# Layer 1's matrices made by halves inside the spectrum's periods, and the weights' products of taps in six instructions

## The chip, the core and the metric

The kernel runs on one NeuronCore of a Trainium2 chip. The metric is the device time of one execution in microseconds; the median of three runs of the kernel before is 4494.61 (4492.34 to 4499.99). The profiled execution spans 4483.5 us. The core's engines are TensorE (PE; PEld is its weight load), VectorE (DVE), ScalarE (ACT), GpSimd (POOL) and SyncE (SP), which issues the transfers. Everything is in fp32.

## What is computed

The input x has the shape (4, 256, 256, 64). Layer 0 is a spectral block with a convolution behind it; layer 1 is a moving average plus a filter of the low frequencies along one axis, which is linear in x.

```python
# layer 0
h  = pw(layernorm(x), w_te)                     # 64 -> 128 channels
F  = fft2(h)
fc = gelu(pw(concat(real(F), imag(F)), w_fc))   # 256 -> 256
x1 = x + pw(real(ifft2(fc)), w_tp)              # 128 -> 64
d  = gelu(depthwise3x3(pw(layernorm(x1), w_fe), w_dw) + b_dw)
x2 = x1 + pw(d, w_fp)
# layer 1, along axis 1 of x2, for each of the 64 channels c
trend = moving_average(x2, 25)
xf    = rfft(x2 - trend)[:128]
out   = trend + irfft(einsum(xf, w_real[c] + 1j * w_imag[c]))
```

Because layer 1 is linear along its axis, the kernel makes one 256x256 matrix per channel from `w_real[c]`, `w_imag[c]` and the average, and applies it by matmul at the end. There are 64 such matrices. They depend on the weights alone, so that their place in the program is free until layer 1 begins. The depthwise 3x3 convolution and the 1x1 convolution ahead of it are joined in the same spirit: the weights `wc_main` and `wc_half` are products of `w_fe` with sums and differences of the taps of `w_dw`. They too depend on weights alone, and are needed from the first chunk of the convolution on.

## The kernel before

**A matrix of layer 1** takes four operations, defined in `matrices`. `v` (L1108, L1109) is two matmuls with 512 columns into one PSUM bank, one with the real and one with the imaginary weights; `vc` (L1113) copies the bank to SBUF on ScalarE; `mm` (L1119) is four matmuls with 256 columns; `mt` (L1130) adds the average's table `avgT` on VectorE and sends the matrix to DRAM (`m_d`, L1131). In a trace each fp32 matmul has two records.

**The order.** The instructions of TensorE, VectorE, ScalarE and GpSimd stand in an order that is written out by hand; each engine works through its own in order. An order is a text of names; `do(op, k)` brings an operation up to index k, after the ones it follows. A number behind a colon is added to the index of the turn or period. SyncE's transfers are not in these orders: a load takes its place there as soon as its buffer is to be had.

The program has these stages:

- **The starting stage**: 17 turns of the order FIRST. A turn takes two chunks of the first image through the layer norm and the forward transform along the rows (`fl` load, `fq` to `fp` statistics, `fx` scaling on GpSimd, `fa`, `fb`, `fh0`, `fh1` sums and differences, `y0`, `y1` matmuls L435, `yt` copies), and makes three matrices, 51 in all.
- **The weights' pieces**: `prepare` is a generator, whose pieces are taken one at a time. From turn 1 on, FIRST takes one at its head and one in its middle (behind `fm:1`, entry 22 of 44). The pieces of the convolution's weights are copies and sums of taps (L317 to L327), then 24 products (L338), each one instruction of 64x128. The last piece, with the bias and the edges (L344 to L365), is run behind the turns.
- **Between**: four steps, BETWEEN, with one matrix each (51 to 54), beside the last chunks of the starting stage.
- **The spectrum**: periods n = 35 to 70. A period takes one chunk of the forward transform and two pairs of columns through the spectrum: `x` (L540, the transform of the columns), `xs` (L555, copy on ScalarE), `m0`, `m1` (L564, the products with the joined weights), `gc` (L578), `b` (L583), `g` (Gelu, L587), `p` (L593, GpSimd), `z` (L617), `zs`, `w` (L634), `zt`; and one step back: `u` (L666), `us` (L683), `uc` (L696), `uf` (L715). The first `us` copy belongs to n = 38. At n = 35 `yr` (L512) prepares the first, special pair.
- **Periods with and without matrices**: n = 35 to 45 use the order SPECTRUM_AND_MATRIX, which holds one matrix per period (numbers 55 to 63, the operations of one matrix drawn out over two periods). From n = 46 to 70 the order is SPECTRUM, which has no matrices. The pools of the matrices and of `prepare` are closed at n = 46, and the convolution's pool is opened in their place. With that the six first loads of `x_c` (L821) may start.
- **The convolution** beside the spectrum of the next images, from n = 71 on, in the order FULL, and at last **layer 1**, which reads the matrices.

**PSUM** is one pool of eight banks, taken in rotation; the ninth request waits for the readers of the first.

Of the kernel before, what the change touches and what calls it, by code (L numbers as in the profile page):

```python
# [129 lines left out]
def conv_seq_kernel(ctx: ExitStack, tc: tile.TileContext, a: dict, tables: bass.AP, out: bass.AP):  # L130
# [108 lines left out]
    def prepare(prep):  # L239
# [76 lines left out]
        tap = lambda dy: w_dwb.rearrange("p (y x) o -> p y x o", x=3)[:, dy]  # L316
        nc.vector.tensor_copy(w_dwh[:, :, 0], tap(0))  # L317
        nc.vector.tensor_copy(w_dwh[:, :, 3], tap(2))
        yield
        w_mid = prep.tile([P, 3, HID], F32, tag="w_mid", name="w_mid")  # L320
        w_sum = prep.tile([P, 3, HID], F32, tag="w_sum", name="w_sum")
        yield
# [5 lines left out]
        for dst, lo, dx in (  # L328
            (wc_main[0:C, 0], 0, 1),
            (wc_main[C:P, 0], C, 2),  # L330
            (wc_main[0:C, 1], 0, 0),
            (wc_main[C:P, 1], C, 1),
            (wc_half[0:C], 0, 2),
            (wc_half[C:P], C, 0),
        ):
            for k in range(4):
                yield
                nc.vector.tensor_tensor(  # L338
                    dst[:, k], w_feg[lo : lo + C], w_dwh[lo : lo + C, dx, k], ALU.mult
                )  # L340
        yield

        ps = bank("ps_b9")
# [739 lines left out]
    def matrices(pool):  # L1083
# [44 lines left out]
        def third(c):  # L1128
            mt = pool.tile([P, 2, N], F32, tag="mt", name=f"mt_{c}", bufs=3)
            nc.vector.tensor_tensor(mt.rearrange("p t n -> p (t n)"), avgT, pss.pop(c), ALU.add)  # L1130
            nc.sync.dma_start(m_d[c], mt)  # L1131

        load(0)
        return {"v": first, "vc": between, "mm": second, "mt": third}


    CM, CO = 2, 2
# [64 lines left out]
    for b in range(B):  # L1202
# [14 lines left out]
        T0 tt0 tt1 eh:-2 | T1 tt0 tt1 gh:-2 | gm T1 | gh gm T1:1 | em T0 | eh em T0:1  # L1217
        gc_0 gh o1:-2 | gc_1 gh o1:-2 | cf0 gc_0 | cf1 gc_1 | ce0 eh cf0 cf1 | ce1 ce0 | cE ce1
        a0 cE | a1 cE | o0 a0 a1 | o1 a0 a1 | fs0 o0 ft0:-1 | fs1 o1 ft1:-1 | ft0 fs0 | ft1 fs1
        st0 ft0 | st1 ft1 | vc v | mm vc | mt mm  # L1220
    """

    def numbered(text):

        return [(w.split(":")[0], int(w.split(":")[1]) if ":" in w else 0) for w in text.split()]

    follows = {}
    for line in FOLLOWS.replace("\n", "|").split("|"):
# [17 lines left out]
        fx:1 vc:2 vc:1 yt0:-1 yt1:-1  # L1246
    """)

    SPECTRUM_AND_MATRIX = numbered("""
        x:1 fq g1:-1 x z:-2 xs:1 zs:-2 v xs fl:1 p1:-1 w:-2 vc b0:-1 fr fm zt:-2 g0:-1 p0:-1 m0 m1  # L1250
        gc1 y1:-2 u b1 z:-1 gc0 fx:-1 b0 zs:-1 y0:-2 fR g1 w:-1 us fM yt1:-2 fa:-1 g0 mm:-1 m1:1 uc
        p1 m0:1 fb:-1 yt0:-2 gc1:1 b1:1 gc0:1 p0 fh1:-1 mt:-1 fp uf fh0:-1 zt:-1
    """)

    SPECTRUM = numbered("""
        fr m0:-1 x g1:-1 xs p1:-1 gc0:-1 x:1 fq m0 z:-2 b0:-1 y1:-2 xs:1 fm gc0 m1 fR zs:-2 g0:-1
        gc1 w:-2 fx:-1 fl:1 y0:-2 fM zt:-2 b0 p0:-1 fp z:-1 fa:-1 fb:-1 yt1:-2 fh1:-1 u b1 yt0:-2
        zs:-1 us fh0:-1 uc m1:1 w:-1 g0 gc1:1 b1:1 p0 zt:-1 g1 p1 uf
        UL:1 XL:1
    """)  # L1260
    PAIRS = set("x xs m0 m1 gc0 gc1 b0 b1 g0 g1 p0 p1 z zs w zt".split())
    BACK = {"u", "us", "uc", "uf"}
    MATRICES = {"v", "vc", "mm", "mt"}

    BETWEEN = [
        numbered("fl:1 fq fr fR"), numbered("fm fM fp"), numbered("fa:-1 fb:-1 fh0:-1 fh1:-1"),
        numbered("fx y0:-2 y1:-2 yt0:-2 yt1:-2"),
    ]
    AHEAD = len(BETWEEN)
    BESIDE = C - 3 * (S0 // 2) - AHEAD  # L1270

    ops, done = {}, {}

    def do(op, index):

        if op not in ops:
            return
        for k in range(done.get(op, -1) + 1, index + 1):
            for other, at in follows.get(op, ()):
                do(other, k + at)  # L1280
            done[op] = k
            if op in PAIRS:
                if k < B * KH:
                    ops[op](k)
            elif op in BACK:
                ops[op](k)
            elif op in MATRICES:
                if k < C:
                    ops[op](k)
            elif op in forward:  # L1290
                if k < B * FWD:
                    ops[op](k)
            elif k in chunk_at:
                ops[op](chunk_at[k])

    def period(n):
        if any(n - k in chunk_at for k in range(5)):
            names = FULL
        else:
            names = SPECTRUM_AND_MATRIX if n - S0 < BESIDE + 2 else SPECTRUM  # L1300
        for op, at in names:
            base = n
            if op in PAIRS:
                base = 2 * (n - S0)
            elif op in BACK:
                base = n - S0
            elif op in MATRICES:
                base = n - S0 + C - BESIDE
            do(op, base + at)

    def starting(n, prep):

        for i, (op, at) in enumerate(FIRST):
            do(op, (3 if op in MATRICES else 2) * n + at)
            if n and i % (len(FIRST) // 2) == 0:
                next(prep, None)

    with in_order, ExitStack() as right:
        with (
# [7 lines left out]
            with ExitStack() as early:  # L1327
# [12 lines left out]
                do("yt0", FWD - 1)  # L1340
                do("yt1", FWD - 1)
                load_group(0)
                for k, names in enumerate(BETWEEN):
                    do("v", C - BESIDE - AHEAD + k)
                    do("vc", C - BESIDE - AHEAD + k)
                    do("mt", C - BESIDE - AHEAD + k - 1)
                    for op, at in names:
                        do(op, S0 - 1 + at)
                begin(0)
                ops |= spectrum  # L1350
                for n in range(S0, S0 + BESIDE + 2):
                    period(n)
                do("mt", C - 1)
            conv = right.enter_context(tc.tile_pool(name="conv", bufs=2, side="right"))
            ops |= convolution(conv)
            for n in range(S0 + BESIDE + 2, S0 + opened(B - 1) + 2):
                period(n)
        with tc.tile_pool(name="seq", bufs=1, side="left", reuse_waits="tile") as seq:
            mts = [matrix_load(seq, c) for c in range(0, CG, CM)]
# [51 lines left out]
```

## Time and profile before

| | us |
|---|---|
| median of three runs | 4494.61 |
| span of the profiled execution | 4483.5 |
| first and last product of the weights' taps | 92.8, 276.8 |
| `x` of n = 35, first records and the bulk | 311.2, 313.1 |
| `x` of n = 39 | 374.8 |
| `us` of n = 39 | 387.4 |
| `us` of n = 46 | 501.4 |
| `us` of n = 66 | 780.4 |
| `us` of n = 71 | 885.7 |

The page gives for each engine its busy time over the span, and the busy share in 40 slices of 112 us each. The timeline gives single instructions; the idle time ahead of one stands in brackets with the instruction that ended it. From `us` to `us` is one period: 16.0 us from n = 39 to 45, then 18.1 and 14.2, then 13.9 to 14.0 up to n = 66.

### The profile page before, as it was taken

The page shows a single profiled execution, that of the slowest core. Times are in us where ns is not written, and L with a number is a line of the kernel's source. Part 1 is how long each engine was busy: PE and PEld are TensorE (multiplying, and loading weights), DVE is VectorE, ACT ScalarE, POOL GpSimd, SP SyncE. Part 2 cuts the span into 40 slices and gives each one's busy share as a digit, 9 for nine tenths or more (in the row PEclk, how much of TensorE's full clock was granted, in tenths as well). Part 3 has the DMA queues.
Part 4 walks back from the last instruction along what each step waited for, and adds up shares of the span by engine and source line. Part 5 has one row for each costly group of instructions (what it writes and reads, how often), then busy time and mean ns, then how long its engine had stood idle before and what let it go on. Part 6 is the DMA issues. An engine that isn't in the chain of part 4 may idle for free.

```text
span 4483.5 us, 63463 instructions
## 1 busy us (share of the span) xinstructions
PE 4346.1 (97%) x22347; PEld 2220.4 (50%) x22347; DVE 3588.9 (80%) x5483; ACT 2508.6 (56%) x3686; POOL 2773.1 (62%) x1774
## 2 busy tenths in 40 slices
PE   7999999799999999999999999999999999999999
PEld 4444333355555555455555555555555455554444
DVE  7988999899999999999998777777777788862222
ACT  2337788666666666666666666666664334331111
POOL 6868899787777777877777555555554555530000
PEclk9999999999999999999999999999999999999999
DMA  6654655444444444444444333333334333329887
GB/s 189 203 178 134 182 151 152 131 114 134 135 134 135 135 128 137 118 132 132 132 132 118 109 108 95 108 99 95 109 104 144 114 95 91 102 89 332 323 321 270
DMA packets 756581, 655.00 MB, mean 146 GB/s; under 512 B 40141, under 2 KB 649375, under 8 KB 747944
## 3 DMA queue, kind: packets, MB, share of 16 engines
q1 hardware_dynamic: 756264, 650.95, 48.0%
q8 instruction: 178, 2.92, 0.3%
q14 instruction: 139, 1.14, 0.1%
HBM read 364.81 MB, written 286.00 MB: 145 GB/s over the span
## 4 chain that ended last, share of the span: by engine, by line
PE 83%; DVE 6%; POOL 4%; DMA 3%; ACT 2%; issue 2%; SPq 1%; DVEq 0%; ACTq 0%; POOLq 0%
PE ps_h_c L915 19%; PE ps_h_c L934 11%; PE ps_o L1166 9%; PE ps_p L564 9%; PE ps_f_c L990 5%; PE ps_z L617 5%; PE ps_s_c L832 5%; PE ps_u L666 4%; PE ps_x L540 4%; PE ps_y L435 4%; PE ps_t_c L869 3%; PE ps_ft_c L1011 3%; PE ps_zt L634 2%; POOL xb L429 1%; DMA xc<-x_d 1%
## 5 line engine op out<-in xcount | busy, mean ns | idle before, releaser
L593 POOL TENSOR_TENSOR g<-g 128x512 f32<-128x512 f32 (+1 forms) x520 | 736.6, 1428 | 545.3 <-ACT g L587 545.3
L915 PE MATMUL ps_h_c<-td_c,wc_main 128*128 128x512 f32 x2048 | 921.7, 593 | 0.0
L583 DVE TENSOR_TENSOR g<-ps_p,g 128x512 f32<-128x512 f32 x1040 | 692.2, 682 | 43.0 <-ACT g L578 25.0
L587 ACT ACTIVATE g<-g,b_fc 128x1024 f32<-128x1024 f32 (+1 forms) x520 | 586.0, 1147 | 181.5 <-DVE g L583 179.8
L230 POOL TENSOR_TENSOR rstd_c<-var_c,minus_half 128x16 f32<-128x16 f32 x128 | 371.8, 2905 | 466.7 <-DVE var_c L224 456.0
L578 ACT COPY g<-ps_p 128x512 f32<-128x512 f32 (+1 forms) x520 | 301.2, 583 | 462.4 <-PE ps_p L564 446.1
L915 PEld LDWEIGHTS ps_h_c<-td_c,wc_main 128*128 128x128 f32 x2048 | 369.1, 190 | 369.8 <-issue 303.7
L934 PEld LDWEIGHTS ps_h_c<-td_c,wc_half 64*128 64x128 f32 x4032 | 417.0, 187 | 244.4 <-issue 194.4
L564 PE MATMUL ps_p<-xs,wp 64*128 64x512 f32 (+1 forms) x2080 | 513.7, 601 | 23.3 <-ACT xs L555 23.3
L934 PE MATMUL ps_h_c<-td_c,wc_half 64*128 64x128 f32 (+1 forms) x4032 | 515.3, 392 | 4.3 <-POOL td_c L889 4.3
L1166 PE MATMUL ps_o<-xc,mt 128*128 128x512 f32 x1024 | 444.5, 596 | 16.4 <-DMA xc<-x_d 16.4
L230 POOL TENSOR_TENSOR rstd<-var,minus_half 128x16 f32<-128x16 f32 x128 | 382.3, 2987 | 77.6 <-DVE var L224 77.6
L966 DVE TENSOR_TENSOR h_c<-h_c,ps_h_c 128x512 f32<-128x512 f32 x512 | 317.3, 682 | 125.8 <-PE ps_h_c L934 125.7
L983 ACT ACTIVATE h_c<-h_c,b_conv 128x1024 f32<-128x1024 f32 x256 | 280.3, 1145 | 203.3 <-DVE h_c L979 203.2
L1180 DVE TENSOR_SCALAR oc<-ps_o,b_fp 128x512 f32<-128x512 f32 x128 | 96.1, 751 | 362.7 <-PE ps_o L1166 355.8
L429 POOL TENSOR_TENSOR xb<-xt 128x512 f32<-128x512 f32 x224 | 290.4, 1313 | 97.9 <-DVE xt L422 96.2
L959 DVE TENSOR_TENSOR h_c<-h_c,ps_h_c 128x512 f32<-128x512 f32 x256 | 175.6, 686 | 199.2 <-PE ps_h_c L934 189.2
L1166 PEld LDWEIGHTS ps_o<-xc,mt 128*128 128x128 f32 x1024 | 195.1, 191 | 265.2 <-issue 237.9
L540 PEld LDWEIGHTS ps_x<-tab,yb 128*64 128x64 f32 x4064 | 242.9, 139 | 130.5 <-issue 95.0
L617 PE MATMUL ps_z<-g,w_tp 128*64 128x512 f32 x1024 | 280.6, 610 | 22.8 <-POOL g L593 21.8
L1178 ACT ACTIVATE oc<-ps_o,b_fp 128x512 f32<-128x512 f32 x128 | 87.9, 687 | 374.3 <-PE ps_o L1166 273.4
L564 PEld LDWEIGHTS ps_p<-xs,wp 64*128 64x128 f32 x2080 | 196.8, 187 | 178.0 <-issue 123.8
(138 smaller groups left out, 7757.2 us busy)
## 6 DMA issues: line engine op xcount, KB each, us to landing
y_d<-yt SPq DMA_DIRECT2D x256, 256.0 KB, 2.5
yb<-y_d SPq DMA_DIRECT2D x256, 256.0 KB, 3.5
u_d<-ut SPq DMA_DIRECT2D x256, 256.0 KB, 4.3
x_c<-in_x_dram SPq DMA_DIRECT2D x128, 512.0 KB, 5.7
x_d<-st SPq DMA_DIRECT2D x128, 512.0 KB, 4.8
xc<-x_d SPq DMA_DIRECT2D x64, 1024.0 KB, 7.1
out_dram<-oc SPq DMA_DIRECT2D x256, 256.0 KB, 3.8
xt<-in_x_dram SPq DMA_DIRECT2D x504, 128.0 KB, 2.8
```

The costliest lines, as they stand in the source:

```text
L230: nc.gpsimd.tensor_tensor(rstd, var, minus_half.to_broadcast([P, n]), ALU.pow)
L429: engine.tensor_tensor(sums[j][:, i], x0, x1, (ALU.add, ALU.subtract)[i])
L540: nc.tensor.matmul(ps[r * C : (r + 1) * C, j * N + t * P : j * N + (t + 1) * P], blk[:, t, k, r * C : (r + 1) * C], tb[:, t, :], start=Tru ...
L564: nc.tensor.matmul(ps[:, :nf], wp[rows, cols], rhs[rows], start=True, stop=r == 1 or not pr["special"],)
L583: nc.vector.tensor_tensor(gt[:, i], re, gt[:, 1], op)
L587: nc.scalar.activation(g, g, AF.Gelu, bias=b_fc[:, half : half + 1])
L593: nc.gpsimd.tensor_tensor(g[:, 0], g[:, 0], g[:, 1], op)
L617: nc.tensor.matmul(ps[r * C : (r + 1) * C, :nf], w_tp, d[:, :nf], start=True, stop=True)
L915: nc.tensor.matmul(ps, wc_main[:, par, k, :], ts[(*j, k)].rearrange("p j i -> p (j i)"), start=True, stop=False,)
L934: nc.tensor.matmul(pss[k, par][:, s * P : (s + n) * P], wc_half[lo : lo + C, k, :], ts[(*at_q, k)][lo : lo + C, at : at + n, :].rearrange( ...
L966: nc.vector.tensor_tensor(g, g, m, (ALU.add, ALU.subtract)[r])
L1166: nc.tensor.matmul(ps[:, :nf], mts[i // CM][:, i % CM, t, to * P : (to + 1) * P], xc[:, t, :, :, i, :], start=t == 0, stop=t == 1,)
```

## The change

It has two parts. The first spreads the matrices over the spectrum. SPECTRUM_AND_MATRIX is dropped, and all periods from n = 35 to 70 use SPECTRUM. Into it come four new operations, which make half a matrix: `hv` two matmuls with 256 columns (one half `t` of the matrix), `hc` a copy of 128x256, `hm` two matmuls with 256 columns, `ht` an addition of 128x256 and a transfer of 128 KB. A half takes two periods: `hv` and `hc` in the first, `hm` and `ht` in the second. So eight matrices, 56 to 63, are made in 32 periods and one more. BETWEEN gets a fifth, empty step, which makes matrix 55, and the matrices begun there are ended there. The pools of the matrices and of `prepare` now stay open up to n = 67.

The second part is for the starting stage: the four products of each block of the convolution's weights become one instruction of 64x512, with `w_feg` repeated along the free axis, and two other pieces are joined. FIRST takes a piece only in its middle, one per turn, so that all pieces are done within the turns.

```diff
-        yield
         w_mid = prep.tile([P, 3, HID], F32, tag="w_mid", name="w_mid")
...
-            for k in range(4):
-                yield
-                nc.vector.tensor_tensor(
-                    dst[:, k], w_feg[lo : lo + C], w_dwh[lo : lo + C, dx, k], ALU.mult
-                )
+            yield
+            nc.vector.tensor_tensor(
+                dst,
+                w_feg[lo : lo + C].unsqueeze(1).to_broadcast([C, 4, HID]),
+                w_dwh[lo : lo + C, dx],
+                ALU.mult,
+            )
...
+        def first_half(k):
+            c, t = C - BESIDE + k // 2, k % 2
...
+            ps = pss["h", k] = bank(f"ps_v_{c}_{t}")
+            for i, f in enumerate((f1, f2)):
+                nc.tensor.matmul(
+                    ps[:, :N],
+                    w[c - c % CG, i][:, c % CG, :],
+                    f.rearrange("p (r n) -> p r n", n=N)[:, :, t * P : (t + 1) * P],
+                    start=i == 0,
+                    stop=i == 1,
+                )
...
+        def second_half(k):
+            vs, ps = vss.pop(("h", k)), bank(f"ps_m_h_{k}")
+            for r, ic in enumerate((icr, ici)):
+                nc.tensor.matmul(ps[:, :N], vs[:, r], ic, start=r == 0, stop=r == 1)
...
+        st0 ft0 | st1 ft1 | vc v | mm vc | mt mm | hc hv | hm hc | ht hm
...
     SPECTRUM = numbered("""
-        fr m0:-1 x g1:-1 xs p1:-1 gc0:-1 x:1 fq m0 z:-2 b0:-1 y1:-2 xs:1 fm gc0 m1 fR zs:-2 g0:-1
+        hv hm fr m0:-1 x g1:-1 xs p1:-1 ht gc0:-1 x:1 fq hc m0 z:-2 b0:-1 y1:-2 xs:1 fm gc0 m1 fR
...
-        numbered("fx y0:-2 y1:-2 yt0:-2 yt1:-2"),
+        numbered("fx y0:-2 y1:-2 yt0:-2 yt1:-2"), [],
     ]
-    AHEAD = len(BETWEEN)
-    BESIDE = C - 3 * (S0 // 2) - AHEAD
+    BESIDE = C - 3 * (S0 // 2) - len(BETWEEN)
...
-            elif op in MATRICES:
-                base = n - S0 + C - BESIDE
+            elif op in HALF_MATRICES:
+                base = (n - S0 - HALF_MATRICES[op]) // 2
...
-            if n and i % (len(FIRST) // 2) == 0:
+            if n and i == len(FIRST) // 2:
                 next(prep, None)
...
+                do("mt", C - BESIDE - 1)
                 begin(0)
                 ops |= spectrum
-                for n in range(S0, S0 + BESIDE + 2):
+                early_end = S0 + 4 * BESIDE + 1
+                for n in range(S0, early_end):
                     period(n)
-                do("mt", C - 1)
```

## The prediction

> **What bounds the kernel now.** First the page's shares and slices: TensorE has records in 97% of the span, and VectorE stays near 90% up to slice 22. The edit lies in slices 1 to 8, where both rows are high, so the share of the whole span settles nothing.
>
> ```profile
> PE 4346.1 (97%) x22347; PEld 2220.4 (50%) x22347; DVE 3588.9 (80%) x5483; ACT 2508.6 (56%) x3686; POOL 2773.1 (62%) x1774
> PE   7999999799999999999999999999999999999999
> DVE  7988999899999999999998777777777788862222
> ```
>
> Next the busy time of each engine by stage. The columns are the window, its length, then PE, PEld, DVE, ACT and POOL busy, granted clock, DMA share, GB/s. I cut the windows at successive `us` copies (one per period); row 1 is one turn of the starting stage, rows 2 and 3 are periods in the order SPECTRUM_AND_MATRIX (row 3 after the matrices ran out), row 4 holds the change of order, row 5 is a period in the order SPECTRUM.
>
> ```profile
> 206.00:221.40 15.40, 14.40 (x53) 7.63 (x52) 14.98 (x24) 5.76 (x10) 12.76 (x7) 1.00 0.71 212
> ...
> 403.40:419.40 16.00, 15.95 (x94) 7.63 (x93) 14.35 (x22) 12.57 (x21) 12.75 (x8) 1.00 0.52 154
> ...
> 467.30:483.30 16.00, 14.03 (x90) 6.80 (x90) 14.35 (x22) 11.98 (x20) 12.75 (x8) 1.00 0.47 140
> 483.30:501.40 18.10, 14.77 (x78) 5.32 (x76) 15.57 (x21) 11.95 (x21) 16.55 (x9) 0.81 1.04 327
> ...
> 557.40:571.40 14.00, 13.11 (x82) 5.28 (x84) 13.28 (x20) 11.94 (x19) 13.22 (x9) 1.00 0.50 139
> ```
>
> The reader is to see that the two orders differ by 2 us a period, and that the longer one stays at 16.00 even without matrix work (row 3): TensorE fills 15.95 us where there is such work, and after it the chain of waits through the order itself holds the pace. The short order is nearly balanced: 13.1 to 13.3 us on TensorE, VectorE and GpSimd in 14.0 (mean 13.95).
>
> Last the timeline of one short period (start, duration, engine, operation; in brackets the idle time before it and who ended it):
>
> ```profile
> 560.00 1.97 PE L540 MATMUL ps_x<-tab,yb 128*64 128x128 f32 x32
> ...
> 562.20 0.57 ACT L555 COPY xs<-ps_x 128x512 f32<-128x512 f32 x1
> ...
> 562.82 1.13 PE L564 MATMUL ps_p<-xs,wp 64*128 64x512 f32 x4 [0.85 <-ACT xs L555]
> ...
> 565.77 0.77 DVE L217 SCALAR_TENSOR_TENSOR var<-total 128x16 f32<-128x16 f32 x1
> ...
> 568.59 1.29 DVE L402 TENSOR_TENSOR xb<-xt 128x512 f32<-128x512 f32 x2 [0.52 <-PE ps_y L435]
> ```
>
> TensorE has one hole of 0.85 us a period, between `x` and the first `m`; otherwise it runs end to end. The hole isn't made by `x`: its first half ends near 561.0, and `xs` starts at 562.20 because two Gelus hold ScalarE from 559.89 to 562.29. So matmuls placed ahead of `x` can push `x` later into this hole.
>
> **What the Trainium skill says.** "Perfetto Trace Analysis", Optimization Strategy, advises interleaving regimes that contend for different engines; here the trace shows only 0.85 us of room per period, so whether it pays is a matter of place. "SBUF — State Buffer", Who interferes with whom: a VectorE instruction with two SBUF inputs and a GpSimd instruction that reads SBUF exclude each other, one input from PSUM doesn't. The trace agrees for the weights' products and the scaling L237; the product ends with it (94.62 and 94.47):
>
> ```profile
> 92.57 1.90 POOL L237 TENSOR_TENSOR xt<-xt,rstd 128x1024 f32<-128x1024 f32 x1
> ...
> 92.78 1.84 DVE L338 TENSOR_TENSOR wc_main<-w_feg,w_dwh 64x128 f32<-64x128 f32 x1
> ```
>
> An unblocked product took 0.28 (101.03), while `mt` (avgT and PSUM) never exceeds 0.69. "VectorE: DVE Perf Modes", The TRN2 errata, gives (N+151)/0.96 ns for an fp32 tensor_tensor: 691 at N=512, and L402 shows 691 on average.
>
> **Part 1: the weights' products, starting stage.** Out: 24 of 64x128, 16 with mean 973 and 8 with mean 854 = 22.4 us of VectorE. In: 6 of 64x512. Each stands in the middle slot of a turn, the one where L237 blocks (92.78); the cheap slot at the head of the turn is dropped. Bounds for one: 0.69 free (L422's row, and the page's formula), 0.69 + 1.56 (1.84 less 0.28) = 2.25 blocked. I take blocked, 13.5, since the slot is the same: 9 us less VectorE. Each remaining turn is also near TensorE's floor: three matrices at 3.75 (below) and four `y` of 0.93 are 15.0, while turns take 15.4 to 17.6. So only part comes through. The last piece (b9, edges), which now stands alone behind the stage and takes TensorE from 286.86 to 289.53, moves into turn 13; its round trip over VectorE costs there about what it cost (the hole was 0.77). I take **-5** for the stage, range -12 to 0.
>
> **Part 2: one more matrix ahead of the spectrum.** `v` starts its two matmuls 0.96 apart (441.49, 442.45): 1.92. `mm` runs 450.96 to 452.78: 1.82. The fifth BETWEEN step has nothing beside it, and a drain follows: TensorE gets `v` 55, `mm` 54 and `mm` 55 = 1.92 + 2 x 1.82 = 5.56 before `x` of the first period, which now waits from 309.2 for `yr`, itself behind `mt` on VectorE. I take **+5.5** in full; 4 if the drain overlaps.
>
> **Part 3: spectrum periods, the main term.** Of the order with matrices 11 periods vanish; all 36 use SPECTRUM, 33 with a half step. Even periods add `hv` and `hc`, odd ones `hm` and `ht`. TensorE: `hm` is half an `mm`, 0.91; `hv` is two matmuls of 256 columns, 0.91 by the `mm` rate, up to 0.96 by `v`. In-order TensorE then has 13.1 + 0.91 = 14.0 us. They stand ahead of `m0:-1` and `x`: first `x` ends at 561.0 + 0.91 = 561.9, before `xs` can start at 562.20; both `x` end near 562.9, and `m0` starts 0.1 late instead of 0.9. Queued behind them is all of TensorE, hence this check decides.
>
> ScalarE gets `hc`, 128x256 from PSUM: 0.35 (`xs` at 256 columns is 0.352), every other period behind the square, and finds the idle 0.30 ahead of L578 at 564.99. VectorE gets `ht`, 0.42 (L422 at 128x256 is 0.416), every other period ahead of `b0:-1`. L217 further on is held 0.6 us by L237 anyway (0.77 against a median of 0.175), so the delay is swallowed there; the 0.52 ahead of L402 is a second reserve. Banks: each period takes 18 of the 8 rotating PSUM banks, now 19. The new one is reused by `y1`, which must wait for `hc` (about 564.55) or `ht` (563.8), and starts at 564.8: no wait.
>
> So 13.95 becomes 14.05 (14.2 if VectorE's mean +0.2 shows). From the `us` of n = 39 (387.4) to that of n = 66 (780.4) are 27 periods and 393.0 us; after, 27 x 14.05 = 379.4: **-13.6**. Ahead of that, `x` at 313.1 to `x` of n = 39 at 374.8 is 61.7 for four filling periods; at 14.4 each 57.6: **-4**.
>
> **Part 4: what the freed pool starts.** The conv pool opens at n = 68 instead of 46, and with it the six `x_c` loads of 512 KB. Row 4 above is that burst (327 GB/s): 18.1 + 14.2 against 2 x 13.95 is 4.4 us, which part 3 has counted as gone. It returns beside the second image's `yr` and the convolution's start: **+4**, from 0 (hidden in the gaps of 796 to 910, where TensorE is busy 91.5 of 114) to 12 if `xt` and `yb` queue behind it in SyncE's order.
>
> Sum: -5 + 5.5 - 13.6 - 4 + 4 = -13.1, so 4494.6 becomes **4481.5**. From n = 71 on nothing changes.
>
> **The rivals.**
> A, the forecast: hole filled, 4481.5.
> B, the half steps add their full 0.91 because `xs` is released by the Gelus, and these by TensorE's delayed `m`: a period of 14.86, 27 x 14.86 = 401.2, +8.2 in place of -13.6; with no gain while filling, +8.2 - 5 + 5.5 + 4 = +12.7, **4507, slower**. Against it: the Gelu ahead of `xs` hangs on `m1:1` at 557.30, which stands ahead of `hv`.
> C, the gain comes but the burst costs 12 at the convolution's start: -5, 4489.5. For it: the critical chain passes through the `xt` loads (2.2 us) in nearly every short period, so they have no slack.
> D, the starting stage falls to TensorE's floor (-12) and the burst hides (0): -24, 4470.5.
>
> **How the numbers follow.** Chances: A 0.52, B 0.12, C 0.20, D 0.16. The bound of 0.2% is 9 us: below 4485.6 lie D and nearly all of A, 0.66; C and the rest of A are within, 0.22; B is above, 0.12. The range takes in A with its unknowns, C, and D down to 4469, and leaves B out: 4469 to 4497.
>
> **What would show it.** After: `us` copies 14.0 to 14.1 apart from n = 39 to 66, the wait of L564 for `xs` near zero, TensorE about 14.0 busy a period; `x` of the first period near 313; products of about 2.2 us; `x_c` loads near 790 us, and the period there longer by some 4. A period of 14.5 or more would refute part 3, products of 0.7 the blocked price; a stall over 8 us near n = 68 would make C true.

## The result, and the profile after

The changed kernel takes 4468.65 us (median of four runs, 4460.64 to 4473.57) against 4493.48 for the kernel before in the same comparison: ratio 0.9943, interval 0.9922 to 0.9964, which is 25 us saved (16 to 35). The forecast was 4481.5 with a range of 4469 to 4497, and the measured time lies just below it. The direction was right, the size was not, and the two parts of the change turned out to pull in opposite directions.

The same rows of the page as were shown of before, now of the changed kernel (busy time, and busy tenths in 40 slices of 112 us). Lines of the code past the new `yield` are moved by one (L564 is now L565, L540 is L541), and L338 is L336.

```profile
PE 4355.5 (97%) x22379; PEld 2222.1 (50%) x22379; DVE 3562.4 (80%) x5473; ACT 2508.7 (56%) x3694; POOL 2777.9 (62%) x1774
PE   7899999799999999999999999999999999999999
DVE  7979999899999999999998777777778788852212
```

VectorE lost 26.5 us of busy time and TensorE gained 9. As before, the shares settle nothing: TensorE stands at 97% in both. The page's groups (line, engine, operation, busy and mean, then idle time ahead of it and who ended most of that) name the place. First the changed kernel, then the kernel before:

```profile
L565 PE MATMUL ps_p<-xs,wp 64*128 64x512 f32 (+1 forms) x2080 | 518.8, 603 | 7.4 <-ACT xs L556 7.4
```

```profile
L564 PE MATMUL ps_p<-xs,wp 64*128 64x512 f32 (+1 forms) x2080 | 513.7, 601 | 23.3 <-ACT xs L555 23.3
```

The 16 us that TensorE used to wait for `xs` are gone. That is the hole of 0.85 us a period that the forecast wanted to fill.

Next the stages of the changed kernel, cut at the same places (window, length, busy time of PE, PEld, DVE, ACT and POOL, granted clock, DMA share, GB/s): two spectrum periods with half steps, then the period in which the second image's work begins (n = 66).

```profile
384.30:398.30 14.00, 13.96 (x86) 5.93 (x88) 13.29 (x21) 11.90 (x19) 13.24 (x9) 1.00 0.58 162
537.70:551.70 14.00, 13.96 (x86) 5.93 (x88) 13.27 (x20) 12.20 (x20) 13.20 (x8) 1.00 0.55 151
760.80:782.10 21.30, 16.65 (x82) 6.45 (x84) 16.03 (x23) 12.11 (x19) 13.34 (x8) 0.84 0.74 238
```

TensorE went from 13.11 to 13.96 busy in windows of the same 14.00 us: 0.85 more work and no more time. From the `us` of n = 39 to that of n = 66 the intervals are 13.94 or 13.95; the one ahead of them, from n = 38 to 39, is 15.0.

The timeline of one such period of the changed kernel (start, duration, engine, operation; idle time in brackets) shows how it fits:

```profile
539.15 1.03 PE L1141 MATMUL ps_v<-t,w 128*128 128x256 f32 x4
540.11 1.13 PE L565 MATMUL ps_p<-xs,wp 64*128 64x512 f32 x4
541.17 1.97 PE L541 MATMUL ps_x<-tab,yb 128*64 128x128 f32 x32
...
542.51 0.57 ACT L556 COPY xs<-ps_x 128x512 f32<-128x512 f32 x1
...
543.13 1.13 PE L565 MATMUL ps_p<-xs,wp 64*128 64x512 f32 x4
544.41 0.37 ACT L1151 COPY vs_h<-ps_v 128x256 f32<-128x256 f32 x1
...
546.07 0.77 DVE L217 SCALAR_TENSOR_TENSOR var<-total 128x16 f32<-128x16 f32 x1
...
548.89 1.29 DVE L403 TENSOR_TENSOR xb<-xt 128x512 f32<-128x512 f32 x2 [0.52 <-PE ps_y L436]
```

`hv` (L1141) pushes `x` to 541.17, its second half ends at 543.14, and `m0` follows at 543.13 with no idle time. `xs` starts 1.34 after `x` where it started 2.20 after it before: `x` came later, `xs` did not: it starts 4.8 us after the period's `us` copy in both kernels. The half's copy takes 0.37. The reserves on VectorE (0.77 at L217, 0.52 at L403) are unchanged.

The profiled executions of either kernel differ by several microseconds among themselves, so four of each were laid side by side (further executions of both are among the experiments). Means, in us, cut at the last `mt` of the turns, the first record of `x` of n = 35, and the `us` of the periods named (differences of the unrounded means):

| stage | before | after | difference | forecast |
|---|---|---|---|---|
| start to the last `mt` of the turns | 290.9 | 297.2 | +6.3 | -5 |
| to `x` of n = 35 | 18.6 | 24.5 | +5.9 | +5.5 |
| to `us` of n = 39 | 75.7 | 63.6 | -12.0 | -4 |
| to `us` of n = 66 | 394.6 | 376.4 | -18.1 | -13.6 |
| to `us` of n = 71 | 107.4 | 108.3 | +0.9 | +4 |
| to layer 1 | 3132.0 | 3132.7 | +0.7 | 0 |
| layer 1 | 465.9 | 468.6 | +2.7 | 0 |
| sum | | | -13.7 | -13.1 |

The sum of the profiled executions agrees with the forecast, but by errors that cancel, and it isn't the timed difference of 25. The granted clock accounts for the larger part of that disagreement. Sorted by their granted clock, the timed spans are 4490.9, 4484.1 and 4482.7 on average for before (at 0.991, 0.992, 0.993) and 4470.6, 4466.3 and 4462.8 for after (six executions in all): some 4 us for a thousandth of the clock, and 18 to 20 us between the kernels at an equal clock. The four profiled executions of before were granted 0.99175 on average, those of after 0.99125; the timed runs of before 0.9908 and those of after 0.9922. An estimate from these figures: at an equal clock the change is worth 16 to 20 us, and the rest of the 25 comes with a clock that was a little over a thousandth higher in the timed runs. Whether the kernel earns that clock or these few runs met it by chance was not settled.

The table hides one more thing. In the traces the granted clock is either full or half, and half mostly for stretches of 3.4 or 6.8 us, which fall at mostly the same places in all executions of one kernel. What a stage loses by them (its length times 1 less the granted share, an upper bound where TensorE waits anyway) is 6.3 us before and 9.0 after in the starting stage, and 4.3 before and nothing after between the `us` of n = 39 and that of n = 66, each a mean of four. By this estimate up to 2.6 of the +6.3 and 4.3 of the -18.1 are TensorE's clock.

### The profile page after: what moved, and what is told of

It reads as the page before. It is cut to its first block, busy times and chain, and to the rows that moved or that the text cites. A ratio compares the mean times of both kernels' runs of the same rounds, so it can differ in the third digit from the quotient of the medians.

```text
span 4471.8 us, 63546 instructions
## 1 busy us (share of the span) xinstructions
PE 4355.5 (97%) x22379; PEld 2222.1 (50%) x22379; DVE 3562.4 (80%) x5473; ACT 2508.7 (56%) x3694; POOL 2777.9 (62%) x1774
## 4 chain that ended last, share of the span: by engine, by line
PE 87%; DVE 4%; POOL 3%; DMA 2%; ACT 2%; issue 1%; SPq 1%; DVEq 0%; POOLq 0%; ACTq 0%
PE ps_h_c L916 19%; PE ps_h_c L935 11%; PE ps_p L565 9%; PE ps_o L1200 9%; PE ps_z L618 5%; PE ps_u L667 5%; PE ps_f_c L991 5%; PE ps_x L541 5%; PE ps_s_c L833 5%; PE ps_y L436 4%; PE ps_ft_c L1012 3%; PE ps_t_c L870 3%; PE ps_zt L635 2%; DMA xc<-x_d 1%; PE ps_m L1120 1%
## 5 line engine op out<-in xcount | busy, mean ns | idle before, releaser
L565 PE MATMUL ps_p<-xs,wp 64*128 64x512 f32 (+1 forms) x2080 | 518.8, 603 | 7.4 <-ACT xs L556 7.4
L541 PEld LDWEIGHTS ps_x<-tab,yb 128*64 128x64 f32 x4064 | 241.9, 138 | 129.8 <-issue 92.1
L618 PE MATMUL ps_z<-g,w_tp 128*64 128x512 f32 x1024 | 282.3, 613 | 22.1 <-POOL g L594 20.8
L436 PE MATMUL ps_y<-xb,tab 128*64 128x512 f32 x1024 | 259.3, 612 | 26.9 <-POOL xb L430 26.1
```

What stands on the lines that cost most here:

```text
L436: nc.tensor.matmul(ps[i * C : (i + 1) * C], dh[:, m, i * C : (i + 1) * C], sums[j][:, i], start=True, stop=True,)
L541: nc.tensor.matmul(ps[r * C : (r + 1) * C, j * N + t * P : j * N + (t + 1) * P], blk[:, t, k, r * C : (r + 1) * C], tb[:, t, :], start=Tru ...
L565: nc.tensor.matmul(ps[:, :nf], wp[rows, cols], rhs[rows], start=True, stop=r == 1 or not pr["special"],)
L618: nc.tensor.matmul(ps[r * C : (r + 1) * C, :nf], w_tp, d[:, :nf], start=True, stop=True)
```

## The experiments

The theory after the result: the halves give more than all of the gain, because TensorE had a hole for them; the joined products cost time, because they left a cheap place for a dear one. The rival: each part gives some of the gain, and where the halves stand doesn't matter.

**The changed kernel again, timed in five rounds**, without an edit, and single executions of both kernels.

> The changed kernel as it is, in five rounds, to separate what the change does from what differs between runs. Theory (the trace pair of before and after agrees with -16.6 us up to the end of the spectrum; the rest of the measured -24.8 is spread of the last stage, layer 1, whose instructions are the same): the median difference comes out between -13 and -20 us, and the time from the first ps_o matmul to the end differs between profiles by several us in either direction. Rival (layer 1 itself gains, for instance because the matrices lie otherwise in DRAM): -22 to -28 again, and a layer 1 stage at least 5 us shorter than in the kernel before.

Measured: 4467.30, ratio 0.9943 (0.9928 to 0.9958). The first result holds, and the 13 to 20 us that were expected are missed: the gain is 24.8. The rival named that size, but not for its reason: layer 1 takes 465.5 us in this profile and 465.8 in that of before.

> The kernel before as it is, for a second profile. Theory (its first profile was a quick one, at 4485.3 where the median of 43 runs is 4492.1): its span is 4 to 10 us longer, the difference lies in turns of the starting stage and in layer 1 where TensorE is granted half its clock, and n = 66 to 71 takes 108 us; periods of 16.0 and 13.94 as before. Rival (n = 66 to 71 takes 105.3 again): the changed kernel does lose 3 us there.

> The kernel before once more, for where its time differs between executions. Theory (the timed runs' difference of 25 us is 18 to 20 us of program and the rest granted clock: the two profiles of before were quick executions, at 0.992, where its runs average 0.991): spans between 4477 and 4500 us, and where it is longer than in the quick profiles the extra lies in turns of the starting stage or in layer 1, each with an interval of half clock in it; periods of 15.97 and 13.94 unchanged. Rival (the profiled execution is quicker as such): 4476 to 4484 again, at a clock of 0.992.

> As the third profile of the kernel before: spans between 4477 and 4500 us by the theory of the granted clock, 4476 to 4484 by the rival.

> The changed kernel once more, likewise. Theory: its two profiles, 4470.9 and 4471.8, were slow executions; spans between 4459 and 4472, and the end of its spectrum's last period before the convolution (n = 71) lies between 862 and 872 us, according to how many turns of the starting stage met half clock. Rival (profiled executions of it are always slow): 4470 to 4473 again, n = 71 at 869 to 873.

> As the third profile of the changed kernel: spans between 4459 and 4472 us by the theory of the granted clock, 4470 to 4473 by the rival.

Measured: 4478.51, 4488.81 and 4494.52 for the kernel before, 4466.02 and 4480.23 for the changed one. The end of the turns lay at 285.8 to 294.1 before and at 296.1 to 299.6 after: the turns of the changed kernel are longer in every pairing. (In the experiments below, it lies at 289.4 and 291.7 in two kernels with the old pieces in their old places, and at 295.1 to 298.6 in four with the changed ones.) Against what was expected, the second profile of before was quicker than the first and one of the changed kernel's spans was longer than expected, 4478.4; that n = 66 to 71 takes 108 us in before came true in three of its four profiles, the first has 105.3. Layer 1, whose instructions are the same in both, took 460.7 to 475.2; its granted clock was 1.00 in the quickest and 0.98 in the slowest. A difference of 5 us between two single profiles of a whole program is therefore no evidence here; the same difference in one stage of all of them is.

**The halves alone**: the old 24 products and both places in a turn, with the new spectrum.

```diff
+            for k in range(4):
+                yield
+                nc.vector.tensor_tensor(
+                    dst[:, k], w_feg[lo : lo + C], w_dwh[lo : lo + C, dx, k], ALU.mult
+                )
...
-            if n and i == len(FIRST) // 2:
+            if n and i % (len(FIRST) // 2) == 0:
```

> The halves alone; the weights' products and their places as in the kernel before (24 of 64x128, two slots in a turn, the last piece behind the turns). Theory (the joined products bring nothing, since turns are held by the wait for GpSimd's lock and by TensorE): as fast as the changed kernel or up to 4 us faster; third addition of turn 16 near 293 us, x of n = 35 near 318; periods 13.94. Rival (the products' 9 us do come through): 5 us slower than the changed kernel.

**The weights alone**: the kernel before, with the six joined products and one place per turn.

```diff
+            yield
+            nc.vector.tensor_tensor(
+                dst,
+                w_feg[lo : lo + C].unsqueeze(1).to_broadcast([C, 4, HID]),
+                w_dwh[lo : lo + C, dx],
+                ALU.mult,
+            )
...
-            if n and i % (len(FIRST) // 2) == 0:
+            if n and i == len(FIRST) // 2:
```

> The weights' products alone; the matrices as in the kernel before. Theory: no gain, 0 to +4 us against the kernel before; mean of L217 in the turns rises from 0.25 to over 0.5 us, so that the lock is waited for there. Rival (the forecast's -5): 5 us faster, x of n = 35 near 306.

Measured: halves alone 4459.87, ratio 0.993 (0.9913 to 0.9947); weights alone 4498.72, ratio 1.0015 (1.0006 to 1.0023). Against the 4492.1 of before in that comparison this is -32.2 and +6.6, together -25.6; both at once gave -24.8. The two parts add up within the noise. By stage the halves alone give +3.8 (to `x`), -13.1, -18.1 and +0.7 (to `us` of n = 71). They have the lowest median of all kernels tried. Their lead over the changed kernel, 7.4 us where up to 4 were expected, has intervals that overlap, but the weights' cost is seen by itself as well, where the interval excludes a ratio of 1. It is more than the 0 to 4 us that were expected; the mean of L217 in the turns rose as expected (0.59 us from turn 2 to 12).

**The halves behind `m1`**: the same instructions, placed where TensorE had no hole.

```diff
-        hv hm fr m0:-1 x g1:-1 xs p1:-1 ht gc0:-1 x:1 fq hc m0 z:-2 b0:-1 y1:-2 xs:1 fm gc0 m1 fR
-        zs:-2 g0:-1 gc1 w:-2 fx:-1 fl:1 y0:-2 fM zt:-2 b0 p0:-1 ...
+        fr m0:-1 x g1:-1 xs p1:-1 gc0:-1 x:1 fq m0 z:-2 b0:-1 y1:-2 xs:1 fm gc0 m1 hv hm fR
+        zs:-2 g0:-1 gc1 w:-2 fx:-1 fl:1 y0:-2 fM zt:-2 hc b0 ht p0:-1 ...
```

> As the changed kernel, but hv and hm stand behind m1, where TensorE runs end to end, instead of ahead of x; hc and ht are moved to idle places behind them. Theory (the halves are free because they fill the hole of 0.85 us between x and m0): the hole comes back, and a period takes 0.8 to 0.95 us longer, 14.75 to 14.9 instead of 13.94; over 33 periods +26 to +31 us against the changed kernel, so slightly slower than the kernel before. Rival (TensorE isn't the bound of a period, the pace is set by VectorE or GpSimd at 13.94): periods stay within 0.2 us of 13.94, and the time within 6 us of the changed kernel.

Measured: 4499.39, ratio 1.0015 (1.0008 to 1.0022), 32 us more than the changed kernel. All its periods from n = 39 to 65 are 14.86 long, the number that rival B of the forecast had worked out for a hole that isn't filled. TensorE's timeline of one period in this kernel:

```profile
541.96 1.13 PE L565 MATMUL ps_p<-xs,wp 64*128 64x512 f32 x4 [1.12 <-ACT xs L556]
544.88 1.13 PE L565 MATMUL ps_p<-xs,wp 64*128 64x512 f32 x4
545.94 1.13 PE L1156 MATMUL ps_m_h<-t,vs_h 128*128 128x256 f32 x4
```

The wait for `xs` is back (1.12), and the half step (L1156) stands at 545.94 and adds its full length. One and the same set of instructions costs 0 or 0.91 us a period by where it stands. The rival, a pace set by VectorE or GpSimd, falls with it.

**Without the halves**: matrices 56 to 63 are not made; eight other matrices are stored a second time in their place.

```diff
-        hv hm fr m0:-1 x g1:-1 xs p1:-1 ht gc0:-1 x:1 fq hc m0 z:-2 b0:-1 y1:-2 xs:1 fm gc0 m1 fR
+        fr m0:-1 x g1:-1 xs p1:-1 gc0:-1 x:1 fq m0 z:-2 b0:-1 y1:-2 xs:1 fm gc0 m1 fR
...
+            if C - 2 * BESIDE <= c < C - BESIDE:
+                nc.sync.dma_start(m_d[c + BESIDE], mt)
```

> As the changed kernel, but matrices 56 to 63 aren't made: the half steps are left out of the periods, and eight other matrices are stored a second time in their place. It prices the 33 half steps. Theory (they lie in the hole of 0.85 us and cost nothing): periods of 13.94 with a wait of 0.85 us of the first m for xs, and the time within 3 us of the changed kernel. Rival (forecast's 0.1 us a period): 3 to 5 us faster, periods of 13.85.

Measured: 4467.18, beside 4467.30 of the changed kernel; the ratio is 0.9959 (0.9945 to 0.9974), against a time of before of 4488.44 in this comparison. The time from n = 39 to 66 is 376.3 without the halves and 376.5 with them. The timeline of this kernel shows the hole open again:

```profile
541.52 1.97 PE L541 MATMUL ps_x<-tab,yb 128*64 128x128 f32 x32
544.33 1.13 PE L565 MATMUL ps_p<-xs,wp 64*128 64x512 f32 x4 [0.84 <-ACT xs L556]
```

So in these 27 periods the halves cost 0.2 us, nothing that can be told from zero, and the period of 13.94 is not set by TensorE's sum of work, though it is 13.96 busy with the halves. Outside them this one profile is shorter than the changed kernel's mean, by 1.4 us in the filling periods and by 2.4 from n = 66 to 71; the `x_c` loads come at 326.5 in this kernel, so that the second difference needn't be the halves'.

**Two halves a period**: each period takes `hv`, `hc`, `hm` and `ht`, and the matrices are done in half as many periods.

```diff
-                base = (n - S0 - HALF_MATRICES[op]) // 2
+                base = n - S0 - HALF_MATRICES[op]
```

> As the changed kernel, but a half step of each kind in every period, so that the 16 halves are made in the first 17 periods of the spectrum (hv and hm both ahead of x: 1.82 us of TensorE a period in place of 0.91). Theory (the hole of 0.85 us is all the room there is): the 16 periods take 13.94 + 1.82 - 0.85 = 14.9 us, the later ones 13.94; +13 to +17 us against the changed kernel. Rival (what matters is only that the order SPECTRUM is used, not how much stands in it): 13.94 throughout, the same time.

Measured: 4474.98, ratio 0.9966 (0.9952 to 0.9979), some 8 us more than the changed kernel. The periods with two halves last 14.75, those after them 13.94. TensorE's timeline of this kernel:

```profile
443.29 1.03 PE L1141 MATMUL ps_v<-t,w 128*128 128x256 f32 x4
444.16 1.03 PE L1156 MATMUL ps_m_h<-t,vs_h 128*128 128x256 f32 x4
...
446.17 1.97 PE L541 MATMUL ps_x<-tab,yb 128*64 128x128 f32 x32
448.07 1.13 PE L565 MATMUL ps_p<-xs,wp 64*128 64x512 f32 x4
```

The first half step fills the hole; the second finds little of it left and costs 0.81 of its 0.91. The hole is as large as one half step and 0.1 us. The loss is smaller than the 13 us and more that had been expected, since only the eleven intervals from n = 39 on pay it: 11 x 0.81 is 8.9, which is what the stage from n = 39 to 66 lost (385.3 against 376.4); the filling periods took no longer (63.1 against 63.6).

**The kernel before with its pool opened late**, to move the burst of `x_c` loads away from n = 46 without the halves.

```diff
+                for n in range(S0 + BESIDE + 2, S0 + 33):
+                    period(n)
...
-            for n in range(S0 + BESIDE + 2, S0 + opened(B - 1) + 2):
+            for n in range(S0 + 33, S0 + opened(B - 1) + 2):
```

> The kernel before, but the pools of the matrices and of prepare stay open up to n = 67, and the convolution's pool with its x_c loads comes at n = 68. It tells what the burst costs at each place. Theory of the forecast (4.4 us at n = 46, and as much again at n = 68): the period of 18.1 us at n = 46 becomes 14 to 15.5, n = 66 to 71 takes 3 to 5 us longer, and the time is that of the kernel before within 3 us. Rival (the late burst is hidden beside the second image's start, since the kernel with the weights alone also takes 108 us from n = 66 to 71 with the burst at n = 46): 3 to 5 us faster than the kernel before, and 108 us from n = 66 to 71 here too.

Measured: 4489.77, ratio 1.0001 (0.9992 to 1.001). The edit didn't do what it was for. The loads of this kernel, by their source line (durations min, median and max in ns, then first and last start):

```profile
L821 SPq DMA_DIRECT2D x_c<-in_x_dram x128: 372/483/1757, 481.0 to 3939.6; - x128
```

They begin at 481.0, as in the kernel before (483.1), though the pool is opened 22 periods later in the program. The transfer of the last matrix stands at 477.3, so that the loads seem to follow the last use of the matrices' memory. So this run can't separate the burst from the change of order. Another kernel can be read for it, because its burst fell among ordinary periods. In the kernel with two halves a period the six loads came at 555.6 to 569.0:

```profile
L822 SPq DMA_DIRECT2D x_c<-in_x_dram x6: 368/480/762, 555.6 to 569.0; - x6
```

and the periods around them are 13.93 to 13.95. There the burst costs nothing. In the changed kernel it comes at 756.9 to 770.5, and the stretch from n = 66 to 71 is 0.9 us longer on average than in before; against the three profiles of before that take 108.0 to 108.2 there, it is 0.2.

**The joined products in both places of a turn**: the changed kernel, with a piece at the head of the turn as well.

```diff
-            if n and i == len(FIRST) // 2:
+            if n and i % (len(FIRST) // 2) == 0:
```

> As the changed kernel, with the six joined products, but a piece at the head and in the middle of a turn as before the change, so that all pieces are done by turn 7. It tells whether the products' joining or the lone slot in the middle costs the 7 us by which the halves alone are faster. Theory (the slot: the first pieces, each a round trip from VectorE to TensorE, cost about 2 us more each in the middle slot): turns 1 and 2 last 18 and 17 us again instead of 19.9 and 19.1, and the time lies within 3 us of the halves alone, so 4 to 8 us under the changed kernel. Rival (the joined product itself, or the wait for the lock that it hands to L217): within 2 us of the changed kernel.

**The same, with the last piece (bias and edges) after the turns**, in the first period of the spectrum:

```diff
+            if n == S0 and (op, at) == ("m0", 0):
+                for _ in pieces:
+                    pass
...
+                if taken[0] < 12:
+                    taken[0] += 1
+                    next(prep)
...
-                for _ in pieces:
-                    pass
```

> As the kernel with joined products in two slots, but the last piece (bias and edges, two round trips between TensorE and VectorE) is taken in the first period of the spectrum ahead of m0, where VectorE and TensorE wait for ScalarE anyway, instead of in a turn. Theory (the piece makes its turn 5 us longer, 20.8 in place of 15.5, for it stalls VectorE, TensorE and then GpSimd's loop): x of n = 35 is 4 to 6 us earlier, the first period at most 2 us longer; 3 to 5 us faster than with the piece in a turn. Rival (the turn's length comes back in the first period, whose waits are longer than its idle time): no gain.

Measured: 4465.44 (0.9947, 0.9934 to 0.9959) and 4465.22 (0.9942, 0.9929 to 0.9954), within 2 us of the changed kernel. The time doesn't bear out the theory that the place of the pieces alone made the loss: with both places turn 2 takes 18.0 again, but the next five take 20.1, 19.1, 17.5, 18.8 and 22.0, and all turns after them, which hold no piece, 15.2 to 16.0. What the pieces gain in later turns they lose in the early ones. One reservation: in the first kernel's profile TensorE lost 11.9 us to half clock from turn 2 to 16, where the changed kernel's four profiles lost 6.8 to 8.5 and those of before 3.4 to 8.3, so that at an equal clock the place might have paid.

**The halves alone, with the last piece after the turns**: the two edits shown above, with 31 pieces in the turns.

> The halves alone, with 24 products in two slots as before the change, and the last piece taken in the first period of the spectrum ahead of m0. Theory: turn 16 lasts about 15.5 instead of 20.7 us, 3 to 5 us faster than the halves alone. Against the joined products with the late piece it shows what the joining brings by itself: theory 0 to 3 us for the joining, for turns are held by GpSimd and TensorE and not by VectorE's load; rival (VectorE's 17 us count) 8 us or more.

Measured: 4461.99, ratio 0.9935 (0.9922 to 0.9948), no gain over the halves alone. The last turn falls from 20.7 to 15.9, but `x` of n = 35 comes at 311.2 where it came at 314.0, and `us` of n = 39 at 376.5 against 376.7: half of what the turn gave back is gone by `x`, the rest goes in the first periods. Against the joined products with the late piece (0.9942) the 24 small ones are 3 us quicker, with intervals that overlap: the joining by itself brings nothing.

## Why the prediction was right in direction and wrong in size

By part, the forecast gave the halves -8 (parts 2 to 4) and the weights -5 (part 1); alone they measured -32 (-22 to -26 at an equal granted clock) and +7. Each term of the first sum was sized too unfavourably, and the term of the second had the wrong sign. In the sum of the profiles these errors cancel, so that its agreement with the forecast is luck. The terms follow one by one.

**The period (part 3, forecast 14.05, measured 13.94).** The mechanism is shown: the halves fit into the hole ahead of `m0` (0 us there, 0.91 elsewhere, 0.81 for a second one). The forecast's 0.1 for a late `m0` was too careful: `m0` follows `x` without idle time, and the period did not grow. 27 periods by 0.11 is 3.0 of the 4.5 us by which the term came out better; the rest is that the kernel before took 394.6 on average and not the 393.0 of the one profile that the forecast worked with.

**The filling periods (forecast -4, measured -12).** After the starting stage this term missed most. Part of it lay in plain sight. TensorE's timeline at the first `x` of the kernel before:

```profile
311.19 0.43 PE L540 MATMUL ps_x<-tab,yr 128*64 128x128 f32 x2 [1.96 <-DVE yr L512]
313.09 1.76 PE L540 MATMUL ps_x<-tab,yr 128*64 128x128 f32 x13 [1.47 <-DVE yr L512]
```

and of the changed kernel:

```profile
319.57 1.03 PE L1141 MATMUL ps_v<-t,w 128*128 128x256 f32 x4
320.71 1.18 PE L541 MATMUL ps_x<-tab,yr 128*64 128x128 f32 x15
```

Before, TensorE idled 3.4 us there for `yr`; it does so in all four profiles of before and with the weights alone, and in none of the four of the changed kernel, nor with the halves alone. Part of the additional matrix (5.5 us) now runs in that time. The forecast saw the wait and still charged the matrix in full; the first part of the wait (1.96) lies ahead of the cut at `x` of n = 35, the second behind it. The rest is that the short order fills faster than the 14.4 a period that was assumed: from the first `x` to that of n = 39 the kernel before took 63.6 (311.2 to 374.8) and the changed one 52.1 (320.7 to 372.8), with the first two `x` only 10.1 apart. The mean of these four is 13.0, below the 13.94 of the full period, while the forecast had set them above it.

**The starting stage (part 1, forecast -5, measured +6.3).** This term missed most. The step that failed is that less work of VectorE comes partly through as time. The forecast took 2.25 for a product, blocked in a slot that stays the same; in the turns of the changed kernel the groups by form (busy, mean ns, idle) show them cheaper:

```profile
L217 DVE SCALAR_TENSOR_TENSOR var<-total 128x16 f32<-128x16 f32 x22 | 12.6, 573 | 0.4
L336 DVE TENSOR_TENSOR wc_main<-w_feg,w_dwh 64x512 f32<-64x512 f32 x4 | 4.3, 1065 | 0.1
L336 DVE TENSOR_TENSOR wc_half<-w_feg,w_dwh 64x512 f32<-64x512 f32 x2 | 1.5, 774 | 0.0
```

Of before, the line that matters in the same view:

```profile
L217 DVE SCALAR_TENSOR_TENSOR var<-total 128x16 f32<-128x16 f32 x24 | 6.1, 253 | 0.4
```

The slot was the same, but not who is first in it. Of the 24 products in the four profiles of the changed kernel, 17 start 0.1 to 0.3 us ahead of the scaling L237 and take 0.70 to 0.83, and the scaling beside them takes 2.34 or 2.35 in place of 1.90; the other seven start behind it and take 1.99 to 2.38. The forecast's blocked price of 2.25 was about right, for the few that pay it.

The products fell from 22.4 to 5.8 us, yet L217, also of two SBUF inputs, rose from 253 to 573 ns. What the page "SBUF — State Buffer", Who interferes with whom, of the Trainium skill says of two such inputs and a GpSimd instruction that reads SBUF fits: in the changed kernel's timeline an L217 that starts at 235.32 and takes 0.85 ends at 236.17, and the scaling L237 on GpSimd, which started at 234.25, ends at 236.15. So it seems that VectorE, relieved of the product, comes earlier to the next instruction that GpSimd's scaling locks out, and waits there; this one case shows it, for the others it is read from the mean. The stages of both kernels, cut at the `mt` of turn 1 and at the last (columns as above), first before, then after:

```profile
44.10:293.00 248.90, 225.67 (x793) 118.81 (x793) 233.07 (x355) 88.11 (x136) 194.14 (x90) 0.98 0.66 198
```

```profile
43.20:296.10 252.90, 226.00 (x794) 118.29 (x794) 226.84 (x342) 87.18 (x134) 195.97 (x90) 0.97 0.63 192
```

VectorE is 6.2 us less busy in a stage that is 4.0 us longer (1.7 of them by the granted clock, by the estimate above). The waits of VectorE in the turns of the changed kernel (engine and line, what it waited for, us in total, times, longest) say where it stands still:

```profile
DVE w_feg L311 <- PE ps_feg L310: 3.7, 1, 3.7
DVE wp L296 <- PE ps_wp L293: 3.7, 1, 3.7
```

Before, these were 0.7 and 2.7. The pieces that go to TensorE and back now stand in the middle of turns 2 and 3, and these turns take 19.9 and 19.1 in place of 18.1 and 17.2 (the fourth profile of the changed kernel has 18.3 for turn 2). In all four, turn 3 holds a stretch at half clock that it has in none of the four of before: 1.7 of its 1.9 us. TensorE's waits of the changed kernel show the other end:

```profile
PE ps_y L436 <- POOL xb L430: 21.5, 11, 2.8
```

against

```profile
PE ps_y L435 <- POOL xb L429: 14.1, 11, 2.7
PE ps_feg L310 <- DVE w_feg L308: 3.5, 1, 3.5
```

in the kernel before: TensorE waits 7.4 us longer for the chunks that pass through VectorE's statistics and GpSimd, and no longer waits 3.5 for `w_feg`, which leaves 3.9. Many turns take 15.2 to 16.0, with a product in them or without a piece, in either kernel, so the forecast's remark that turns are near their floor was right and should have set the term to nothing at best. That there is a loss is shown, by the weights alone and by every profile. That the round trips make it is read from these waits and not shown: with both places in use the time is no better. How the 6 us divide among round trips, the lock and the clock stays open.

The front section and part 1 say that the last piece stood behind the turns before. It didn't: in the order it is in the middle of turn 16, and that turn takes 20.5 to 21.2 in the profiles of before. In the changed kernel it is in turn 13, which takes 20.5 to 20.8. The claim that it costs the same in either place holds.

**The additional matrix (part 2, forecast +5.5).** Measured +5.9 at `x`, +3.8 with the halves alone; the weights alone make +2.2 there, which the forecast didn't have. As said above, part of the matrix runs in the wait for `yr`.

**The burst (part 4, forecast +4, measured +0.9).** The step that failed is the reading of row 4: the loss of 4.4 us at n = 46 was put down to the loads. Row 4 itself shows a granted clock of 0.81, and 0.19 of 18.1 us is 3.4 of these 4.4. In the other three profiles of before, two or three periods up to n = 46 take 17.6 to 17.9 us at a granted clock of 0.90, the earlier of them ahead of the loads; in the changed kernel the clock is 1.00 from n = 39 to 66 in all four. So most of that loss is TensorE's clock and not the loads, and it didn't come back with them; the same six loads among ordinary periods cost nothing. Why the clock falls there is open: these are the periods of the old order in which the matrices run out, but since order and burst could not be separated in the kernel before, that the order makes it is argued, not shown.

**The rivals.** B's period of 14.86 is what the halves behind `m1` show, so it was a real case, though there for want of a hole and not because the Gelus came late; comparing the end of `x` with the start of `xs` was the right way to decide it. C did not happen. D came nearest in its total. It was right that the burst hides and wrong in its main reason: the starting stage did not fall by 12 but rose.

## What to carry to other kernels

In an order that is fixed by hand, what a piece of work costs is decided by the hole it stands in: find the engine's idle time per period in the timeline, ask who ends it and whether that moves when something is placed ahead, and size the piece to the hole. Fewer and larger instructions were no gain here, on an engine whose freed time went into other waits; before joining small pieces, make sure that this engine sets the length of the turn, and keep pieces that make a round trip through another engine where neither side waits. When a part of a change can be measured alone, measure it: here one part hid a loss inside the other's gain.

## What the runs showed of the hardware

A product of 64x512 with both inputs in SBUF took 0.67 to 0.72 us when free; in the kernel with both places in use its median is 1.49 and its maximum 2.38 (durations min, median, max in ns; first and last start):

```profile
L336 DVE TENSOR_TENSOR wc_main<-w_feg,w_dwh x4: 674/1488/2379, 85.1 to 112.9; 64x512 f32<-64x512 f32 x4
```

Where the product starts 0.1 to 0.3 us ahead of GpSimd's scaling it takes 0.70 to 0.83, and the scaling 2.34 or 2.35 instead of 1.90; where it starts behind, it takes 1.99 to 2.38 and the scaling 1.90 (24 products in the four profiles of the changed kernel).

The mean granted clock of the kernel before lay between 0.989 and 0.993 from execution to execution, with mean spans of 4499.1 and 4482.7 at the two ends: two thirds of the effect studied. It is lost mostly in stretches of 3.4 or 6.8 us at half clock, and a change of schedule can add or remove such stretches (from n = 39 to 66 none in the four profiles after, one to three in those of before). And the instructions of layer 1, equal in both kernels, took from 460.7 to 475.2 us, so that the end of a program says less of an early edit than the stage in which the edit lies.
